# Strided pairs for the moving operand and the bank: the fp32r pass of a GRU's gate matmuls on TensorE

## The chip, the cores and the metric

The kernel runs on one NeuronCore of a Trainium2 chip. The metric is the device time of one launch in microseconds (us); lower is better. A second number that appears below is the span of the profiled execution, from its first to its last instruction.

## The reference

64 graphs of 256 nodes with 256 features each. Two layers, both of the form `x = x + layer(relu(layernorm(x)))`:

```python
# layer 0: gated graph network, 3 rounds, A = (adj != 0)
for i in range(3):
    m = h @ weight[i]
    aggr = A.T @ m                      # per graph
    gi, gh = aggr @ w_ih.T + b_ih, h @ w_hh.T + b_hh
    r, z = sigmoid(gi_r + gh_r), sigmoid(gi_z + gh_z)
    n = tanh(gi_n + r * gh_n)
    h = (1 - z) * n + z * h
# layer 1: graph attention, one head
h = relu(layernorm(x)) @ W.T
e = leaky_relu(h @ a_left [:, None] + h @ a_right [None, :])
x = x + softmax(where(adj == 0, -1e9, e)) @ h
```

All inputs and the output are fp32 (`adj` is int32).

## The kernel before

**Tiling.** Two graphs make a pair, so a tile is 128 partitions by 512 columns (2 graphs of 256 nodes). There are 32 pairs. The features lie on the partitions, in two blocks of 128 (`DB` = 2), and the nodes along the free dimension.

**Three passes in place of fp32.** A value `v` is split into three tiles by `split16` (L662 to L679) or `limbs`: a tile of the class `round` with dtype fp32r (4 bytes an element[...]), and two fp16 tiles of the class `half` (the remainder, and a scaled copy). The weights are split in the same way in the setup: `fac[m]` is fp32r, `low[m]` holds two fp16 parts; `m` is "hh" for the hidden weights, 0, 1 or 2 for the product of `weight[i]` and the input weights, "W" for the attention layer. A product is then one fp32r matmul (j = 0) and two fp16 matmuls (j = 1, 2) for each block of 128 contracted features, all added up in one PSUM bank of 512 fp32 columns.

**The gates.** `gate` (L704) takes a bank and runs `passes` (L698) for the terms it is given: `hs`, the split of the state h, against `fac_hh` and `low_hh`, and `gs`, the split of the aggregated neighbours g, against the factor of the round. For one pair and one round there are, for each of the two output blocks, the gates r (h and g), nh (h), ni (g) and z (h and g), so 6 terms, each with 2 contracted blocks and 3 passes: 12 fp32r matmuls with h and 12 with g for a pair and round. Over 32 pairs and 3 rounds this gives 1152 of each. In the last pair the rounds 1 and 2 are done for each graph by itself, with twice as many matmuls of 256 columns. The profile counts 1128 of 512 columns and 48 of 256 for h, and as many for g. The line that issues them is L701:

```python
return [(j, lambda start, j=j, kb=kb: nc.tensor.matmul(bank.t[:, cols], fs(j, kb), s[kb][j].t[:, cols], start=start, stop=True,
                                                       skip_group_check=True)) for kb in range(DB) for j in range(3)]
```

In this call the first operand is the bank that is written, the second is the stationary operand (128 columns of a factor), and the third is the moving operand, streamed column by column from SBUF. All three are contiguous runs in each partition.

**Who reads the bank.** ScalarE takes r and z with a tanh (L859, L872), scales nh in place (L723); VectorE takes nh and ni (L864, L867). They read the bank contiguously.

**Other fp32r matmuls.** The propagation along A (`prop`, L840) and the attention layer (`mix` L1005, `project` L1024) use fp32r and 16-bit passes too. The plain fp32 matmuls are few: the setup (L639) and the last pair.

**Order.** `Plan.run` is a list scheduler in Python: it places every operation by estimated cost, priorities and hand-set leads (`LEAD`), with pools of buffers for the classes (28 `full`, 22 `round`, 40 `half`, 8 `bank`). It decides the order of the instructions on each engine when the kernel is built. The costs that it uses for a gate, `PASS` = 233 ns for an fp32r pass of 512 columns and `PASS16` = 216 ns for a 16-bit one, are constants of the kernel.

**A copy that reads from two places.** For the transposes through DMA, `dma_turn` and `join` (L744 to L748) move 16-bit halves of fp32 values. `join` is a ScalarE copy of 1024 elements of 2 bytes that reads alternately from two planes of the source and writes contiguously:

```python
dst.t.bitcast(U16).rearrange("p (j n b) -> p j n b", j=2, b=2),
src.t.bitcast(U16).rearrange(f"p ({order}) -> p j n b", j=2, b=2)   # order: "b j n" or "j b n"
```

Of the kernel before, what the change touches and what calls it, by code (L numbers as in the profile page):

```python
# [372 lines left out]
def tile_gated_gnn_then_gat(  # L373
# [39 lines left out]
    nc = tc.nc  # L413
# [281 lines left out]
    def columns(part):  # L695
        return slice(part[0] * N, (part[-1] + 1) * N)

    def passes(bank, cols, m, es, s, first):  # L698

        fs = lambda j, kb: fac[m][:, kb, es] if j == 0 else low[m][:, j - 1, kb, es]  # L700
        return [(j, lambda start, j=j, kb=kb: nc.tensor.matmul(bank.t[:, cols], fs(j, kb), s[kb][j].t[:, cols], start=start, stop=True,  # L701
                                                               skip_group_check=True)) for kb in range(DB) for j in range(3)]

    def gate(name, e, terms, tops, apart=False, bias=None, part=ALL):  # L704

        bank = Buf("bank")
        half = e // 3
        cols, cost, cost16 = columns(part), PASS if len(part) == 2 else PROP, PASS16 if len(part) == 2 else PROP16

        def go(terms, first):  # L710
            seq = [q for m, s in terms for q in passes(bank, cols, m, ts(e, P), s, first)]
            seq.sort(key=lambda q: ((1, 2, 0) if narrow[0] else (0, 1, 2)).index(q[0]))
            for n, (j, run) in enumerate(seq):
                run(first and n == 0)

        for ts_ in [terms[:1], terms[1:]] if apart and len(terms) > 1 else [terms]:
            early = len(ts_) < len(terms) and ts_[0] is terms[0]
            tops.append(pe(name + " top" + str(early)[0], 2 * (cost + 2 * cost16) * len(ts_),
                           lambda ts_=ts_: go(ts_, ts_[0] is terms[0]), mixed=True,
                           r=[(s[kb][j], part) for _, s in ts_ for kb in range(DB) for j in range(3)] + [  # L720
                               (f"fac{m}", tuple((kb, half, j) for kb in range(DB) for j in range(2))) for m, _ in ts_], w=[(bank, ONE)]))
        if bias is not None:
            act(name + " scale", fit(575, part), lambda: nc.scalar.activation(  # L723
                bank.t[:, cols], bank.t[:, cols], AF.Identity, bias=bias), r=[("b_nh", ONE)], w=[(bank, ONE)])
        return bank
# [395 lines left out]
```

## Time and profile before

| | |
|---|---|
| median of 2 runs | 1945.63 us (1944.67 to 1946.6) |
| the profiled execution | 1943.53 us, of which its span is 1941.7 us |
| TensorE busy (PE, matmuls) | 1930.5 us, 99% of the span |
| weight loads (PEld) | 1216.4 us, 63% |
| VectorE (DVE) | 1650.8 us, 85% |
| ScalarE (ACT) | 1593.6 us, 82% |
| GpSimd (POOL) | 171.2 us, 9% |
| granted TensorE clock | 0.999 of full speed |

How to read the profile's rows: "L701 PE MATMUL bank<-round,fac_hh 128\*128 128x512 f32" is a matmul issued by line 701, which writes a bank from a moving `round` tile and the stationary `fac_hh`; fp32r operands show as f32. Behind the bar stand the busy time of the group, the mean duration of one instruction in ns, and the idle time of the engine ahead of it. The duration of a matmul contains the way through the pipeline, so durations of neighbours overlap; the price of a matmul in a dense stream is the distance between starts, which the timeline shows.

### The profile page before, as it was taken

The numbers are of one execution on the slowest core, as the hardware profiler recorded it, in microseconds if no ns is written. First come the engines' busy times: TensorE is split into PE (matmuls) and PEld (weight loads), VectorE is DVE, ScalarE is ACT, GpSimd is POOL, SyncE is SP. The second block draws the span as 40 slices with busy tenths as digits, with TensorE's granted clock in tenths as the row PEclk, the third lists the DMA queues.
The fourth block names the chain that finished last, engine by engine and source line by source line (L and its number), as shares of the span: only waits on it lengthen the run. The fifth ranks groups of instructions, "written<-read, shape, count | busy, mean of one in ns | idle before, by whom it ended". The sixth has DMA issues, their size and how long they took to land.

```text
span 1941.7 us, 31443 instructions
## 1 busy us (share of the span) xinstructions
PE 1930.5 (99%) x10288; PEld 1216.4 (63%) x10288; DVE 1650.8 (85%) x3972; ACT 1593.6 (82%) x2789; POOL 171.2 (9%) x262
## 2 busy tenths in 40 slices
PE   9999999999999999999999999999999999999998
PEld 6655666666666666666666666666666666666677
DVE  7677889888889888898888898888898888988887
ACT  6567888888888888888888888888888888888876
POOL 2001011010011010110010110101110101100000
PEclk9999999999999999999999999999999999999999
DMA  4138766676665676765666665677656765657543
GB/s 142 24 92 129 136 126 126 112 143 136 136 127 113 128 141 134 136 127 108 138 141 136 123 128 115 142 136 129 135 115 127 141 136 133 122 113 140 119 77 71
DMA packets 734469, 239.43 MB, mean 123 GB/s; under 512 B 658256, under 2 KB 734304, under 8 KB 734304
## 3 DMA queue, kind: packets, MB, share of 16 engines
q1 hardware_dynamic: 734272, 237.41, 62.3%
q8 instruction: 80, 1.31, 0.3%
q14 instruction: 85, 0.70, 0.1%
q10 hardware_dynamic: 32, 0.01, 0.0%
HBM read 61.09 MB, written 16.84 MB: 40 GB/s over the span
## 4 chain that ended last, share of the span: by engine, by line
PE 96%; DVE 1%; DMA 1%; ACT 1%; issue 0%; SPq 0%; ACTq 0%; DVEq 0%
PE bank L701 77%; PE bank L840 9%; PE bank L1024 4%; PE bank L1005 4%; PE bank L639 1%; DMA full<-full 0%; DMA x<-in_x_dram 0%; DMA full<-line 0%; DMA full<-in_L_gnn_w_hh_dram 0%; DVE full L939 0%; DVE small L761 0%; PE bank L1066 0%; PE bank L911 0%; PE bank L1074 0%; PE bank L1035 0%
## 5 line engine op out<-in xcount | busy, mean ns | idle before, releaser
L701 PE MATMUL bank<-half,low_hh 128*128 128x512 f16 (+1 forms) x2352 | 623.3, 376 | 0.1
L701 PE MATMUL bank<-half,low 128*128 128x512 f16 (+1 forms) x2352 | 616.2, 376 | 0.0
L701 PE MATMUL bank<-round,fac_hh 128*128 128x512 f32 (+1 forms) x1176 | 404.3, 437 | 0.0
L746 ACT COPY full<-full 128x1024 uint16<-128x1024 uint16 x304 | 350.5, 1164 | 54.3 <-DMA full<-full 50.0
L701 PE MATMUL bank<-round,fac 128*128 128x512 f32 (+1 forms) x1176 | 394.1, 426 | 0.1
L701 PEld LDWEIGHTS <-low 128*128 128x128 f16 x2352 | 216.8, 98 | 261.5 <-issue 44.1
L701 PEld LDWEIGHTS <-low_hh 128*128 128x128 f16 x2352 | 206.3, 98 | 259.9 <-issue 79.8
L671 DVE SCALAR_TENSOR_TENSOR half<-bank,round 128x512 f16<-128x512 f32 (+1 forms) x254 | 171.7, 685 | 99.5 <-ACT round L669 84.0
L701 PEld LDWEIGHTS bank<-round,fac_hh 128*128 128x128 f32 x1176 | 217.0, 189 | 62.6
L701 PEld LDWEIGHTS bank<-round,fac 128*128 128x128 f32 x1176 | 215.5, 189 | 58.0 <-ACT round L669 0.4
L768 POOL TENSOR_TENSOR small<-small,nhalf 128x2 f32<-128x2 f32 x128 | 100.1, 783 | 1709.2 <-DVE small L766 1705.0
L859 ACT ACTIVATE full<-bank,b_rz 128x512 f32<-128x512 f32 (+1 forms) x196 | 132.3, 675 | 98.3 <-PE bank L701 97.9
L674 ACT ACTIVATE half<-bank 128x512 f16<-128x512 f32 (+1 forms) x254 | 151.2, 595 | 49.0 <-PE bank L1005 28.8
L872 ACT ACTIVATE full<-bank,b_rz 128x512 f32<-128x512 f32 (+1 forms) x196 | 132.2, 674 | 52.2 <-PE bank L701 50.9
L671 DVE SCALAR_TENSOR_TENSOR half<-full,round 128x512 f16<-128x512 f32 (+1 forms) x254 | 169.4, 680 | 5.0 <-ACT round L669 2.4
L864 DVE SCALAR_TENSOR_TENSOR full<-full,bank 128x512 f32<-128x512 f32 (+1 forms) x196 | 131.9, 673 | 40.1 <-ACT full L859 39.4
L723 ACT ACTIVATE bank<-bank,b_nh 128x512 f32<-128x512 f32 (+1 forms) x196 | 127.1, 649 | 44.2 <-PE bank L701 44.1
L669 ACT ACTIVATE round<-full 128x512 fp32r<-128x512 f32 (+1 forms) x254 | 152.7, 629 | 11.2 <-DVE full L880 10.3
L878 DVE SCALAR_TENSOR_TENSOR full<-full,full 128x512 f32<-128x512 f32 (+1 forms) x196 | 132.4, 676 | 33.1 <-ACT full L872 32.3
L688 DVE SCALAR_TENSOR_TENSOR half<-full,round 128x512 f16<-128x512 f32 x184 | 126.2, 687 | 25.0 <-ACT round L687 24.9
L669 ACT ACTIVATE round<-bank 128x512 fp32r<-128x512 f32 (+1 forms) x254 | 144.5, 598 | 1.0 <-PE bank L840 0.8
L876 DVE TENSOR_TENSOR full<-full,full 128x512 f32<-128x512 f32 (+1 forms) x196 | 130.6, 678 | 17.0 <-ACT full L869 17.0
(114 smaller groups left out, 2547.4 us busy)
## 6 DMA issues: line engine op xcount, KB each, us to landing
full<-full SPq DMA_DIRECT2D x484, 128.0 KB, 3.4
x<-in_x_dram SPq DMA_DIRECT2D x64, 256.0 KB, 3.1
adj<-in_adj_dram SPq DMA_DIRECT2D x64, 256.0 KB, 4.7
full<-in_x_dram SPq DMA_DIRECT2D x64, 256.0 KB, 4.9
full<-full SPq DMA_DIRECT2D x248, 64.0 KB, 2.5
out_dram<-full SPq DMA_DIRECT2D x62, 256.0 KB, 4.0
full<-line SPq DMA_DIRECT2D x62, 128.0 KB, 4.5
full<-full SPq DMA_TRANSPOSE x304, 3.2
```

The lines of the kernel that those rows point to most:

```text
L669: act(f"{name} 0{of}", cut(A512 if bank else C512), lambda: nc.scalar.activation(v0.t[:, cols], v.t[:, cols], AF.Copy, scale=up), r=[(v, h ...
L671: dve_(f"{name} 1{of}", cut(V512), lambda: nc.vector.scalar_tensor_tensor(v1.t[:, cols], v.t[:, cols], up, v0.t[:, cols].bitcast(F32), op0 ...
L674: act(f"{name} d{of}", cut(A512), lambda: nc.scalar.activation(vd.t[:, cols], v.t[:, cols], AF.Copy, scale=up * unit), r=[(v, has)], w=[(v ...
L701: return [(j, lambda start, j=j, kb=kb: nc.tensor.matmul(bank.t[:, cols], fs(j, kb), s[kb][j].t[:, cols], start=start, stop=True, skip_gro ...
L723: act(name + " scale", fit(575, part), lambda: nc.scalar.activation(bank.t[:, cols], bank.t[:, cols], AF.Identity, bias=bias), r=[("b_nh", ...
L746: act(name, 1065, lambda: nc.scalar.copy(dst.t.bitcast(U16).rearrange("p (j n b) -> p j n b", j=2, b=2), src.t.bitcast(U16).rearrange(f"p ...
L840: nc.tensor.matmul(pa.t[:, ts(g, N)], b, m[:, ts(sb, N)], start=(n == 0), stop=True, skip_group_check=True)
L859: act(f"r {db}{of}", fit(575, part), lambda b=r_, k=pr, db=db, cols=cols: nc.scalar.activation(b.t[:, cols], k.t[:, cols], AF.Tanh, bias=b ...
L864: dve(f"u {db}{of}", fit(S512, part), lambda u=u, k=ph, b=r_, cols=cols: nc.vector.scalar_tensor_tensor(u.t[:, cols], b.t[:, cols], 1.0, k ...
L872: act(f"z {db}{of}", fit(575, part), lambda b=z_, k=pz, db=db, cols=cols: nc.scalar.activation(b.t[:, cols], k.t[:, cols], AF.Tanh, bias=b ...
L876: dve2(f"d sub {db}{of}", fit(V512, part), lambda u=u, d=d, cols=cols: nc.vector.tensor_sub(d.t[:, cols], d.t[:, cols], u.t[:, cols]), r=[ ...
L878: dve2(f"d mul {db}{of}", fit(V512, part), lambda d=d, b=z_, cols=cols: nc.vector.scalar_tensor_tensor(d.t[:, cols], b.t[:, cols], 1.0, d. ...
```

## The change

The matmuls with j = 0 in `passes` (fp32r by fp32r) stream the moving tile in another order of columns and write the bank's columns in that same order, so that each column of the result lands where it did before. The 16-bit passes, the weights, and every reader of the bank stay as they are.

```diff
+    WEFT = {"hh": "p (l q e) -> p q l e", 0: "p (l q e) -> p q l e", 1: "p (l q e) -> p q l e", 2: "p (q l e) -> p l q e"}
+    STEP = {"hh": 4, 0: 4, 1: 8, 2: 2}
+
     def passes(bank, cols, m, es, s, first):
 
+        weft = lambda t, m, j: t.rearrange(WEFT[m], q=STEP[m], e=2) if j == 0 else t
         fs = lambda j, kb: fac[m][:, kb, es] if j == 0 else low[m][:, j - 1, kb, es]
-        return [(j, lambda start, j=j, kb=kb: nc.tensor.matmul(bank.t[:, cols], fs(j, kb), s[kb][j].t[:, cols], start=start, stop=True,
+        return [(j, lambda start, j=j, kb=kb: nc.tensor.matmul(
+            weft(bank.t[:, cols], m, j), fs(j, kb), weft(s[kb][j].t[:, cols], m, j), start=start, stop=True,
                                                                skip_group_check=True)) for kb in range(DB) for j in range(3)]
```

In all cases the innermost run is a pair of neighbouring elements (8 bytes). What follows a pair differs:

| m | pattern of 512 columns | distance to the next pair | matmuls of 512 / of 256 columns |
|---|---|---|---|
| hh | 4 x 64 x 2 | 32 bytes | 1128 / 48 |
| 0 | 4 x 64 x 2 | 32 bytes | 384 / 0 |
| 1 | 8 x 32 x 2 | 64 bytes | 372 / 24 |
| 2 | 128 x 2 x 2 | 1024 bytes forth, then back to the pair beside the first | 372 / 24 |

(With 256 columns the counts in the middle halve, and the distance for m = 2 is 512 bytes.) In the first three patterns the row of pairs is run through from end to end, and then again 8 bytes further on. Every engine has the same instructions in the same order as before; the scheduler's costs are not touched.

## The prediction

> **What bounds the kernel now.** I read the page's busy times first, then the chain that ended last, then the waits of TensorE, and last the timeline for the price of one matmul.
>
> ```profile
> PE 1930.5 (99%) x10288; PEld 1216.4 (63%) x10288; DVE 1650.8 (85%) x3972; ACT 1593.6 (82%) x2789; POOL 171.2 (9%) x262
> ...
> PE 96%; DVE 1%; DMA 1%; ACT 1%; issue 0%; SPq 0%; ACTq 0%; DVEq 0%
> ...
> L701 PE MATMUL bank<-round,fac_hh 128*128 128x512 f32 (+1 forms) x1176 | 404.3, 437 | 0.0
> L746 ACT COPY full<-full 128x1024 uint16<-128x1024 uint16 x304 | 350.5, 1164 | 54.3 <-DMA full<-full 50.0
> L701 PE MATMUL bank<-round,fac 128*128 128x512 f32 (+1 forms) x1176 | 394.1, 426 | 0.1
> ...
> L669 ACT ACTIVATE round<-full 128x512 fp32r<-128x512 f32 (+1 forms) x254 | 152.7, 629 | 11.2 <-DVE full L880 10.3
> ```
>
> Busy share alone would not do, since matmuls overlap in it. But the chain agrees: 96% of the span is TensorE following TensorE, 77.0% of it L701. The two fp32r rows are the 2352 matmuls that the change touches; their idle time is 0.0 and 0.1 us.
>
> The waits of TensorE, all of the span (us, times, longest):
>
> ```profile
> PE bank L1024 <- ACT round L669: 2.9, 1, 2.9
> PE bank L527 <- POOL ident masks.py:199: 1.4, 1, 1.4
> ```
>
> The nine entries of that answer sum to under 8 us. There is no slack on TensorE: a nanosecond more per matmul goes into the time nearly in full, and the other engines (85% and 82% busy) follow.
>
> The price of one matmul, from the timeline (start, length of the row, what):
>
> ```profile
> 593.27 0.82 PE L701 MATMUL bank<-round,fac_hh 128*128 128x512 f32 x2
> 593.93 0.63 PE L701 MATMUL bank<-round,fac 128*128 128x512 f32 x2
> 594.39 0.63 PE L1024 MATMUL bank<-fac_W,round 128*128 128x256 f32 x4
> 594.87 1.05 PE L1024 MATMUL bank<-low_W,half 128*128 128x256 f16 x8
> 595.75 0.59 PE L701 MATMUL bank<-half,low_hh 128*128 128x512 f16 x2
> 596.18 0.59 PE L701 MATMUL bank<-half,low 128*128 128x512 f16 x2
> ```
>
> From start to start: two fp16 matmuls of 512 columns take 596.18 - 595.75 = 0.43, so 0.215 each; two fp32r ones 594.39 - 593.93 = 0.46, so 0.23. (The first fp32r row after 16-bit ones is recorded early and isn't used.) With 256 columns: fp16 0.88 / 8 = 0.11, fp32r 0.48 / 4 = 0.12. A longer stretch confirms this: the chain has "325.36 16.04 PE bank L701 x72", and the groups of that window are 48 fp16 and 24 fp32r matmuls: (16.04 - 48 x 0.2155) / 24 = 0.237, changes of kind included. I take 0.233 (0.12 for 256 columns). So the contiguous fp32r stream already runs some 8% below the fp16 stream, and in proportion to its columns[...].
>
> [...]
>
> **What a new line costs, from the trace.** `join` (L746) reads 1024 elements of 2 bytes, alternately from two places[...]. It takes 1164 ns. A contiguous copy of as many elements: L669 takes 632 ns for 512 and 418 for 256 columns (groups by form), a slope of 0.836 ns an element, so 632 + 512 x 0.836 = 1060. [...] TensorE takes an element in 0.42 ns. [...] the alternative, that the fp32r stream is held back by its bytes[...], fits the 8% as well.
>
> **The change part by part.**
> 1. Nothing is removed; instruction counts and order are the same on all engines. The split tiles, the weights (190 ns a load against 233 of a matmul, hidden) and the readers of the bank are untouched.
> 2. hh, 0 and 1: [...] Count: 1128 + 384 + 372 = 1884 of the first kind, 48 + 24 = 72 of the second. 1884 x 0.230 = 433.3, and 72 x 0.115 = 8.3. Bounds: below, no extra at all (0), or a gain of 0.018 for each if the 8% came from the order and vanished; above, 0.230.
> 3. Round 2: pairs go back and forth between two places, as `join` does[...]. I take 0. Upper bound[...]: 372 x 0.230 + 24 x 0.115 = 88.3.
> 4. The bank: [...] I take 0 beside item 2[...]. [...]
> 5. What hides it: nothing on TensorE. The last 23 us of the chain lie mostly on VectorE, so some of the 8.3 us may be covered there; I leave them in.
>
> Sum against the profiled execution's own time: 1943.5 + 433.3 + 8.3 = 2385.1. The median of the runs stands 2.1 higher, so 2387.
>
> **The rivals.**
> - *Pairs are enough (not slower).* [...] Place: every fp32r matmul of L701. Price 0 each: 1945.6. [...] if the 8% vanish, 2256 x 0.018 = 41 less, 1905. [...] For: over its 1024 alternating reads `join` loses only 104 of 1060 ns[...]. [...]
> - *One step a line.* [...] 1884 x 0.104 + 72 x 0.052 = 200, so 2146; with round 2 as well, 2186. [...] Against: TensorE has half the time for an element.
> - *The array's own half rate.* The pairs go at exactly half of fp16's pace, 0.43 instead of 0.233: 1884 x 0.197 + 72 x 0.10 = 378, so 2324; with round 2, 2404. This is inside the forecast's own range.
> - *The bank is worse than the reading*[...]. Nothing in the profile gives a price; if it costs double again, over 2480.
>
> **How the numbers follow.** Doubling of the lines, with or without round 2: 0.48, own range 2310 to 2480. One step a line: 0.17 (2100 to 2200). Pairs are enough: 0.31 (1905 to 1985, mostly at 1946). The bank worse: 0.04. To leave out no more than 2 in 10 the range must reach from the rival at 1946 to the forecast's upper end: 1940 to 2480. Faster by over 2% (about what a measurement of this kernel can tell from no change) would need all of the 8% back and more: 0.01. Within 2%: 0.30. Slower: 0.69.
>
> **What would show it.** In the changed profile the distance between starts of the fp32r matmuls of hh, 0 and 1 should be 0.43 to 0.47 us, those of round 2 (the third large block of gates of a pair) should stay near 0.233, the fp16 ones 0.215, and `prop`, `mix` and `project` 0.12. PE stays at 99%, DVE and ACT fall to about 70% and 66% (1650.8 and 1593.6 over 2385). The prediction is wrong if hh stays at 0.233 (pairs are enough), if it is near 0.34 (one step), or if round 2 is slowed like the others.

## The result and the profile after

The changed kernel takes 2398.43 us (median of 2 runs, 2397.81 to 2399.04) against 1945.63: a ratio of 1.2327, with an interval of 1.2274 to 1.238. The forecast was 2387 us, slower with a chance of 0.69. The profiled execution took 2399.04 us with a span of 2397.2, so the span grew by 455.5 us.

The page after, with busy times, the chain, and the gates' groups (now at L705):

```profile
PE 2389.9 (100%) x10288; PEld 1258.4 (52%) x10288; DVE 1667.9 (70%) x3972; ACT 1626.6 (68%) x2789; POOL 170.8 (7%) x262
...
PE 99%; DMA 0%; DVE 0%; SPq 0%; issue 0%; ACT 0%; ACTq 0%
...
L705 PE MATMUL bank<-round,fac_hh 128*128 128x512 f32 (+1 forms) x1176 | 668.9, 681 | 0.0
L705 PE MATMUL bank<-half,low_hh 128*128 128x512 f16 (+1 forms) x2352 | 628.5, 379 | 0.0
L705 PE MATMUL bank<-half,low 128*128 128x512 f16 (+1 forms) x2352 | 618.9, 377 | 0.0
L705 PE MATMUL bank<-round,fac 128*128 128x512 f32 (+1 forms) x1176 | 601.4, 616 | 0.0
```

The two fp32r groups grew from 404.3 to 668.9 and from 394.1 to 601.4 us; the fp16 groups hardly moved. TensorE's busy time grew by 459.4 us and its idle time fell from 11.2 to 7.3, which together is the 455.5. The other engines have the same work spread over more time (70% and 68%). So the loss lies in the 2352 matmuls that the change touches, and on the path that sets the end.

The timeline after (start, length, what) around two places; the first lies in round 2, the second at the passage from round 1 to round 0:

```profile
919.49 1.09 PE L705 MATMUL bank<-round,fac_hh 128*128 128x512 f32 x2
920.40 0.84 PE L705 MATMUL bank<-round,fac 128*128 128x512 f32 x2
921.08 0.40 PE L705 MATMUL bank<-half,low_hh 128*128 128x512 f16 x1
...
952.74 1.06 PE L705 MATMUL bank<-round,fac 128*128 128x512 f32 x2
953.61 1.12 PE L705 MATMUL bank<-round,fac_hh 128*128 128x512 f32 x2
954.55 1.92 PE L705 MATMUL bank<-half,low_hh 128*128 128x512 f16 x8
956.12 1.27 PE L705 MATMUL bank<-round,fac_hh 128*128 128x512 f32 x2
957.19 1.12 PE L705 MATMUL bank<-round,fac 128*128 128x512 f32 x2
958.13 0.63 PE L705 MATMUL bank<-half,low 128*128 128x512 f16 x2
```

From start to start, for one matmul: hh (32 bytes) (920.40 - 919.49) / 2 = 0.455 and (954.55 - 953.61) / 2 = 0.47; g in round 0 (32 bytes) (958.13 - 957.19) / 2 = 0.47; g in round 1 (64 bytes) (953.61 - 952.74) / 2 = 0.435; g in round 2 (back and forth) (921.08 - 920.40) / 2 = 0.34. Before, all were at 0.23.

### The profile page after: what moved, and what is told of

Read it like the earlier page. It is cut to its first block, busy times and chain, and to the rows that moved or that the text cites. A ratio compares the mean times of both kernels' runs of the same rounds, so it can differ in the third digit from the quotient of the medians.

```text
span 2397.2 us, 31442 instructions
## 1 busy us (share of the span) xinstructions
PE 2389.9 (100%) x10288; PEld 1258.4 (52%) x10288; DVE 1667.9 (70%) x3972; ACT 1626.6 (68%) x2789; POOL 170.8 (7%) x262
## 4 chain that ended last, share of the span: by engine, by line
PE 99%; DMA 0%; DVE 0%; SPq 0%; issue 0%; ACT 0%; ACTq 0%
PE bank L705 83%; PE bank L845 7%; PE bank L1029 3%; PE bank L1010 3%; PE bank L639 0%; DMA x<-in_x_dram 0%; PE bank L1018 0%; DMA full<-in_L_gnn_w_hh_dram 0%; PE bank L1071 0%; PE bank L916 0%; PE bank L1079 0%; PE bank L1040 0%; PE bank L656 0%; PE bank L898 0%; DVE small L766 0%; SPq L555 0%
## 5 line engine op out<-in xcount | busy, mean ns | idle before, releaser
L705 PE MATMUL bank<-round,fac_hh 128*128 128x512 f32 (+1 forms) x1176 | 668.9, 681 | 0.0
L705 PE MATMUL bank<-half,low_hh 128*128 128x512 f16 (+1 forms) x2352 | 628.5, 379 | 0.0
L705 PE MATMUL bank<-half,low 128*128 128x512 f16 (+1 forms) x2352 | 618.9, 377 | 0.0
L705 PE MATMUL bank<-round,fac 128*128 128x512 f32 (+1 forms) x1176 | 601.4, 616 | 0.0
L705 PEld LDWEIGHTS <-low_hh 128*128 128x128 f16 x2352 | 214.8, 104 | 374.7 <-issue 194.2
L705 PEld LDWEIGHTS <-low 128*128 128x128 f16 x2352 | 220.5, 100 | 319.0 <-issue 101.1
L705 PEld LDWEIGHTS bank<-round,fac 128*128 128x128 f32 x1176 | 228.2, 198 | 167.0 <-issue 126.8
L877 ACT ACTIVATE full<-bank,b_rz 128x512 f32<-128x512 f32 (+1 forms) x196 | 133.0, 679 | 267.6 <-PE bank L705 267.6
L705 PEld LDWEIGHTS bank<-round,fac_hh 128*128 128x128 f32 x1176 | 225.4, 196 | 139.3 <-issue 75.5
L872 DVE TENSOR_TENSOR full<-full,bank 128x512 f32<-128x512 f32 (+1 forms) x196 | 131.8, 674 | 79.8 <-PE bank L705 76.3
L874 ACT ACTIVATE full<-full,vec 128x512 f32<-128x512 f32 (+1 forms) x196 | 138.9, 711 | 38.2 <-DVE full L872 36.3
```

Of the source, the lines that this page charges most:

```text
L705: return [(j, lambda start, j=j, kb=kb: nc.tensor.matmul(weft(bank.t[:, cols], m, j), fs(j, kb), weft(s[kb][j].t[:, cols], m, j), start=st ...
L872: dve(f"u add {db}{of}", fit(V512, part), lambda u=u, k=pn, cols=cols: nc.vector.tensor_add(u.t[:, cols], u.t[:, cols], k.t[:, cols]), r=[ ...
L874: act(f"tanh {db}{of}", fit(615, part), lambda u=u, en=en, cols=cols: nc.scalar.activation(u.t[:, cols], u.t[:, cols], AF.Tanh, bias=b_i[: ...
L877: act(f"z {db}{of}", fit(575, part), lambda b=z_, k=pz, db=db, cols=cols: nc.scalar.activation(b.t[:, cols], k.t[:, cols], AF.Tanh, bias=b ...
```

## The experiments

In all kernels below the factors carry names of their own: `fac_hh`, and `fac_first`, `fac_second`, `fac_third` for 0, 1 and 2, so that one run prices four patterns in groups of their own (the matmuls with h, and those with g in rounds 0, 1 and 2). The price per matmul is read as: busy time of the group, less that of the same group with contiguous reading, over the count. (At the seams of groups records overlap, so small differences of this reading are uncertain by a few ns: contiguous `fac_first` reads 132.0 us and, beside the strided fp16 passes below, 133.0, 0.003 each.) The contiguous figures come from the write-only kernel: 393.9 us for `fac_hh` (1128 matmuls of 512 columns), 132.0 for `fac_first` (384), 123.9 for `fac_second` (372) and 128.8 for `fac_third` (372). A pattern is written as in the change, `F` for `"p (l q e) -> p q l e"` and `A` for `"p (q l e) -> p l q e"`, followed by q and e. "Runs" of a pattern are the neighbouring elements that it takes at a visit, its "step" is the distance from one run to the next. Contiguous, a matmul of 512 columns takes 0.215 us from start to start in fp16, and 0.017 more in fp32r, 0.232 (medians of the durations before: 379 and 396 ns).

The expectations speak of lines. A line is here a stretch of the row whose first element costs the stream extra time and whose others come with it. That each pair costs a line of its own was supposed before any run and is not shown by the profile before; what the runs show of a line's price and length is put together after the single elements.

**Reading alone.**

```diff
+    MOVING = {"hh": (F, 4, 2), 0: (F, 4, 2), 1: (F, 8, 2), 2: (A, 2, 2)}
+    BANK = {"hh": None, 0: None, 1: None, 2: None}
-            weft(bank.t[:, cols], m, j), fs(j, kb), weft(s[kb][j].t[:, cols], m, j), start=start, stop=True,
+            weft(bank.t[:, cols], BANK[m], j), fs(j, kb), weft(s[kb][j].t[:, cols], MOVING[m], j), start=start, stop=True,
```

> Only the moving operand of the fp32r gate matmuls is read in the order of the change; the bank is written contiguously, so the columns of these products land in other places than the reference asks for. Theory 'lines of SBUF'[...]: all of the loss stays, about 2400 us, starts 0.46 us apart for the 32-byte step and 0.33 for round 2. Rival 'bank' (the order of writing in PSUM costs it): the loss goes, 1946 us, starts 0.233 apart. If both halve the rate on their own, about 2400 here and in the write-only kernel.

Measured: 2398.43 us, ratio 1.2347 (1.2326 to 1.2368). The groups by form:

```profile
L711 PE MATMUL bank<-round,fac_hh 128*128 128x512 f32 x1128 | 653.0, 692 | 0.0
...
L711 PE MATMUL bank<-round,fac_first 128*128 128x512 f32 x384 | 222.3, 678 | 0.0
...
L711 PE MATMUL bank<-round,fac_second 128*128 128x512 f32 x372 | 200.2, 649 | 0.0
...
L711 PE MATMUL bank<-round,fac_third 128*128 128x512 f32 x372 | 165.6, 548 | 0.0
```

More per matmul: 0.230 us for hh, 0.235 for 0, 0.205 for 1; `fac_third` (round 2) 0.099. All of the loss is in the reading.

**Writing alone.** `MOVING` and `BANK` of the kernel above are exchanged.

> The counterpart: the moving operand is read contiguously, the bank is written in the order of the change, so the columns land in other places. Theory 'lines of SBUF': 1946 us within 0.5%, starts 0.233 us apart. Rival 'bank': about 2400 us, 0.46 apart for the 32-byte step. If the bank costs only beside round 2's back and forth: 1944 + 372 x 0.097 = 1980.

Measured: 1944.08 us, ratio 1.0001 (0.9992 to 1.0009).

```profile
L711 PE MATMUL bank<-half,low_hh 128*128 128x512 f16 x2256 | 608.0, 381 | 0.0
L711 PE MATMUL bank<-round,fac_hh 128*128 128x512 f32 x1128 | 393.9, 442 | 0.0
...
L711 PE MATMUL bank<-round,fac_first 128*128 128x512 f32 x384 | 132.0, 427 | 0.0
L711 PE MATMUL bank<-round,fac_third 128*128 128x512 f32 x372 | 128.8, 440 | 0.0
...
L711 PE MATMUL bank<-round,fac_second 128*128 128x512 f32 x372 | 123.9, 427 | 0.0
```

The 393.9 is that of the kernel before, to the digit. Writing the bank in pairs at steps of 32, 64 or 1024 bytes costs nothing here. The rival "bank" falls.

**Runs of four elements.**

```diff
-    MOVING = BANK = {"hh": (F, 4, 2), 0: (F, 4, 2), 1: (F, 8, 2), 2: (A, 2, 2)}
+    MOVING = BANK = {"hh": (F, 2, 4), 0: (F, 4, 4), 1: (F, 8, 4), 2: (A, 2, 4)}
```

> As the change, with runs of four elements (16 bytes) in place of pairs: steps of 32, 64 and 128 bytes for hh, 0 and 1, back and forth between two places for 2; reading and writing alike. Theory 'lines of SBUF': [...] 1946 us (starts 0.233), at most 1% more. Rival 'any step off the next element costs': half of the pairs' extra for half as many breaks, about 0.35 us a matmul, 2170 us. Rival 'the bank by its step': as the change, 2400.

Measured: 1949.9 us in one run. Per matmul against contiguous: hh (32 bytes) 392.5 us for the group, -0.001; 0 (64 bytes) 127.7, -0.011; 1 (128 bytes) 128.4, +0.012; 2 (back and forth) 135.5, +0.018.

```profile
L711 PE MATMUL bank<-round,fac_hh 128*128 128x512 f32 x1128 | 392.5, 442 | 0.0
...
L711 PE MATMUL bank<-round,fac_first 128*128 128x512 f32 x384 | 127.7, 415 | 0.0
```

A strided stream as such costs next to nothing: with 16 bytes at a time instead of 8 at most 0.018 us a matmul is left of the loss, and at a step of 64 bytes the stream is even quicker than the contiguous one. That was not expected.

**Pairs at other distances.**

```diff
+    MOVING = BANK = {"hh": (F, 2, 2), 0: (F, 16, 2), 1: (F, 32, 2), 2: (F, 64, 2)}
```

> Pairs at other distances: 16 bytes for hh, 128, 256 and 512 bytes for 0, 1 and 2; reading and writing alike. Theory 'lines of SBUF': every pair still fetches a line, whatever the distance, so starts 0.43 to 0.46 us apart for all four, round 2 included, and 1944 + 1128 x 0.229 + 1128 x (0.20 to 0.229) = 2430 to 2460 us. Rival 'even and odd parts'[...]: hh falls to 0.233, so 2170 to 2205 us.

Measured: 2460.12 us in one run. More per matmul: 16 bytes 0.223, 128 bytes 0.240, 256 bytes 0.270, 512 bytes 0.215.

```profile
L711 PE MATMUL bank<-round,fac_hh 128*128 128x512 f32 x1128 | 645.5, 685 | 0.0
```

Pairs about double the matmul at every distance tried (0.215 to 0.270 more on 0.232), the step of 16 bytes included; the rival "even and odd parts" falls. The four prices differ by up to 0.055, but each distance was tried on other matmuls, so this run doesn't say that the distance makes the difference.

**Pairs from several places in turn.**

```diff
+    MOVING = BANK = {"hh": (A, 2, 2), 0: (A, 4, 2), 1: (A, 8, 2), 2: (A, 16, 2)}
```

> Pairs taken in turn from 2 places (hh, 1024 bytes apart), 4 places (0, 512 apart), 8 (1) and 16 (2), and then from the next pair at each place; reading and writing alike. If the two lines last used are kept, 2 places cost 0.33 us a matmul (as round 2 in the change) and 4, 8 and 16 places the full 0.43 to 0.49: 1944 + 1128 x 0.097 + 1128 x 0.22 = 2300 us. If more lines are kept, 4 places (or more) are at 0.33 too: 2050 to 2200. Rival 'no line is kept, jumps of 1024 bytes happen to be cheap': 0.33 for 2 places, and no step between 2 and 4 that goes with the number of places.

Measured: 2311.93 us in one run. More per matmul: 2 places 0.098, 4 places 0.223, 8 places 0.269, 16 places 0.210.

```profile
L711 PE MATMUL bank<-round,fac_hh 128*128 128x512 f32 x1128 | 504.7, 549 | 0.0
...
L711 PE MATMUL bank<-round,fac_first 128*128 128x512 f32 x384 | 217.6, 666 | 0.0
...
L711 PE MATMUL bank<-round,fac_hh 128*128 128x256 f32 x48 | 12.7, 363 | 0.0
```

The jump in price lies between 2 and 4 places. I read it so, as an estimate from the 0.098 and the 0.223: a line is still there if one other was used in between, and gone if three were. The rival "jumps of 1024 bytes happen to be cheap" falls by the matmuls of 256 columns in the same run: their two places lie 512 bytes apart, and they cost (12.7 - 10.4) / 48 = 0.048 more than contiguous, again about half of the price of pairs for 256 columns (0.115), while four places at the same 512 bytes cost the whole of it.

Three of these patterns are those of the run before in other words. A row of 512 columns has 2048 bytes, so pairs at a step of 512, 256 or 128 bytes come from 4, 8 or 16 places in turn. The price of one and the same pattern was thus taken twice: 0.215 (with `fac_third`) and 0.223 (with `fac_first`) for 512 bytes, 0.270 and 0.269 (both with `fac_second`) for 256, 0.240 (with `fac_first`) and 0.210 (with `fac_third`) for 128. What sets the last 0.03 is therefore not the pattern alone.

**The fp16 passes strided.** The fp32r passes stay contiguous; `weft` acts for j = 1 and 2, with

```diff
+    MOVING = BANK = {"hh": (F, 8, 2), 0: (F, 4, 4), 1: (F, 2, 8), 2: (A, 2, 2)}
```

> The fp32r passes are contiguous; in their place both fp16 passes of the gates are strided: pairs of 4 bytes at a step of 32 bytes for hh, runs of four (8 bytes) at 32 bytes for 0, runs of eight (16 bytes) at 32 bytes for 1, pairs back and forth between two places for 2. Theory 'lines of SBUF at 1.67 ns': what counts is the number of lines, not of bytes: hh fetches 256 lines, 0.43 to 0.46 us in place of 0.216; 0 fetches 128, 0.216 to 0.232; 1 fetches 64, 0.216; 2 between 0.216 and 0.33. Sum: 1944 + 2256 x (0.214 to 0.245) + up to 12 + up to 85 = 2430 to 2590 us. [...]

Measured: 2548.66 us in one run.

```profile
L711 PE MATMUL bank<-half,low_hh 128*128 128x512 f16 x2256 | 1152.6, 633 | 0.0
...
L711 PE MATMUL bank<-half,low_third 128*128 128x512 f16 x744 | 240.8, 439 | 0.0
L711 PE MATMUL bank<-half,low_first 128*128 128x512 f16 x768 | 216.4, 396 | 0.0
L711 PE MATMUL bank<-half,low_second 128*128 128x512 f16 x744 | 203.9, 383 | 0.0
```

Contiguous, these groups are at 608.0, 196.6, 203.4 and 201.7 us. More per matmul: pairs (4 bytes) at 32 bytes 0.241; runs of four (8 bytes) 0.017; runs of eight (16 bytes) 0.003; pairs back and forth 0.059. (`fac_hh`, which is contiguous here, also shows more busy time, 439.3 against 393.9 us. I read that as overlap of records with the slower fp16 matmuls: the fp16 groups alone grew by 617 us, the 256-column ones included, which is more than the 603.4 us that the time grew over 1945.22 before on this chip.) Runs of 8 bytes double the fp32r stream and leave the fp16 stream nearly alone, while runs of two elements double both. So it isn't bytes that count, but elements: by the runs so far, two at a visit are too few (0.230 and 0.241 more), and four are enough (at most 0.018 more). The next run narrows this down.

**Single elements, reading alone.**

```diff
+    MOVING = {"hh": (F, 2, 1), 0: (F, 4, 1), 1: (F, 8, 1), 2: (A, 2, 1)}
+    BANK = {"hh": None, 0: None, 1: None, 2: None}
```

> Single fp32r elements, in the reading alone (the bank is written contiguously, so the columns land in other places): steps of 8, 16 and 32 bytes for hh, 0 and 1, single elements back and forth between two places for 2. Theory 'lines at 1.67 to 1.8 ns': hh fetches 256 lines[...], 0.43 to 0.46 us; 0 and 1 fetch 512, 0.86 to 0.92 us; 2 keeps its lines, 0.33. Sum: 1944 + 1128 x 0.22 + 756 x 0.65 + 372 x 0.1 = 2720 us. Rival 'what is not the next element costs the same once, pair or single': 0.46 for 0 and 1 as well, 2400 us.

Measured: 2346.93 us in one run, 370 less than my theory said.

```profile
L711 PE MATMUL bank<-round,fac_hh 128*128 128x512 f32 x1128 | 642.6, 682 | 0.0
...
L711 PE MATMUL bank<-round,fac_first 128*128 128x512 f32 x384 | 222.3, 678 | 0.0
...
L711 PE MATMUL bank<-round,fac_second 128*128 128x512 f32 x372 | 199.9, 649 | 0.0
...
L711 PE MATMUL bank<-round,fac_third 128*128 128x512 f32 x372 | 124.5, 430 | 0.0
```

Singles at 16 bytes (`fac_first`) cost 0.235 more, at 32 bytes (`fac_second`) 0.204: what the pairs cost at 32 and 64 bytes in these groups (222.3 and 200.2 us), though twice as many places are visited. Singles at 8 bytes (`fac_hh`) cost 0.220, as the pairs at 16 bytes did (0.223). And single elements back and forth between two places (`fac_third`) cost nothing; they are 0.012 quicker than the contiguous stream. A price per line visited, the theory so far, can't say this. Nor can the rival of the expectation, by which what is not the next element costs the same each time: from two places in turn no element is the next one.

What can is a model, an estimate of mine from these runs: the columns enter two at a time, and the first and the second of each two are fetched each for itself. I call them two streams, one of the even and one of the odd columns. Each delivers an element in a step of 0.84 ns, two columns at the pace of the fp16 stream (0.215 / 256), and a new line takes it two steps, 1.68 ns: the pairs of the change take 0.435 to 0.47 us, 1.70 to 1.84 ns for each two columns. The length of a line is read from the same runs: in contiguous fp32r the elements of one stream lie 8 bytes apart and keep the pace (0.232 us), in pairs at 16 bytes they lie 16 apart and cost 0.223 more, so I put it at 16 bytes, four fp32r elements. Pairs at 16, 32 and 64 bytes and singles at 8, 16 and 32 bytes then give each stream the same walk, a new line for every element at a step of 16, 32 and 64 bytes; this is why their prices agree three times over. Runs of four give each stream two elements to the line. Singles from two places give each a contiguous run of its own, four elements to the line. The 0.017 by which fp16 in runs of 8 bytes is slower fits too: there each stream has two elements to the line, as in contiguous fp32r, which stands 0.017 above contiguous fp16 (0.232 against 0.215).

**The same elements in two orders.** To try that theory against the one before, the fp32r matmuls of `prop` (256 columns, 768 of them; the gates are as before the change) read two elements from each 16 bytes of the tile's row, 128 lines of the model:

```diff
-                            nc.tensor.matmul(pa.t[:, ts(g, N)], b, m[:, ts(sb, N)], start=(n == 0), stop=True, skip_group_check=True)
+                            nc.tensor.matmul(pa.t[:, ts(g, N)], b, of_block(m, sb, part, lo), start=(n == 0), stop=True, skip_group_check=True)
+                        # of_block, for the fp32r part; for the 16-bit part as before
+                        return m.rearrange("p (l h q e) -> p q l e h", h=2, q=2, e=2)[:, sb]     # A0 B0 A1 B1
+                        return m.rearrange("p (l h q e) -> p q l h e", h=2, q=2, e=2)[:, sb]     # A0 A1 B0 B1, the other kernel
```

> The gates are as before the change. The 768 fp32r matmuls of the propagation read, from all lines of the tile, one half of each (so half of the columns twice over two matmuls' places; the columns are others than the reference asks for): in the order A0 B0 A1 B1, A and B neighbouring lines, then the next two lines. Theory 'two streams' (odd and even columns are fetched each for itself, a line costs each two steps of 0.83 ns): each stream takes two elements in turn from its line, 128 steps of columns, 0.109 to 0.12 us as before, 1946 us. Theory 'one stream, 1.7 to 1.8 ns a line': 128 lines for 256 columns, 0.23 us, 768 x 0.113 = 87 us more, 2032 us.

> The same elements as in the kernel before it, with the same part of the computation changed, in the order A0 A1 B0 B1. Theory 'two streams': each stream needs another line for every element, 0.216 to 0.23 us, 1944 + 768 x (0.097 to 0.113) = 2018 to 2032 us. Theory 'one stream': 128 lines[...], the same 0.23 and 2032 us. If instead both orders stay at 0.117, lines aren't what counts and both are at 1946.

Measured: 1945.23 us for A0 B0 A1 B1 and 2026.11 for A0 A1 B0 B1, one run each, against 1947.04 before on the same chip. The lines of `prop` from the one and the other, as minimum / median / maximum of the durations in ns:

```profile
L845 PE MATMUL bank<-round,round x768: 277/278/363, 23.7 to 1914.0; 128*128 128x256 f32 x192
```

```profile
L845 PE MATMUL bank<-round,round x768: 388/421/472, 22.0 to 1995.0; 128*128 128x256 f32 x192
```

Against the first order the second adds 80.9 us over 768 matmuls, 0.105 each; the first adds nothing to the time before. The same elements, in the same groups of four columns, cost once or nearly twice by their order alone: once where, in the model, each stream takes its two elements in turn from one line. One stream with a price per line would have given 2032 for both.

**Longer runs.**

```diff
+    MOVING = BANK = {"hh": (F, 2, 8), 0: (F, 4, 8), 1: (F, 4, 16), 2: (F, 16, 4)}
```

> Longer runs of fp32r elements, reading and writing alike: 32 bytes at a step of 64 for hh, 32 bytes at 128 for 0, 64 bytes at 256 for 1, 16 bytes at 256 for 2. All fetch 128 lines, so by the number of lines alone all take 0.216 to 0.235 us, 1920 to 1950 us in sum. What is beyond 1.67 ns a line goes with the step by the runs so far (runs of 16 bytes: 0.232 at 32 bytes, 0.221 at 64, 0.243 at 128): if a step of 64 bytes is what helps, hh is at 0.221 to 0.232; if a step of 256 hurts, 2 is at 0.245 or more, and 1 between.

Measured: 1958.59 us in one run. Per matmul against contiguous: 32 bytes at 64: -0.001 (392.7 us for the group); 32 at 128: -0.003; 64 at 256: +0.005; 16 at 256: +0.043. The number of lines alone doesn't settle what is left. In the same group, `fac_third`, 16 bytes at a step of 256 cost 0.043, and the next run has 16 bytes at 64 at 0.008 below contiguous, so the step has a part in it. Since reading and writing had the same step here, and the writing alone was never tried at 128, 256 or 512 bytes, the run can't say whether the step hurts the reading or the writing.

**A version that beats both.** Runs of four at 64 bytes for all fp32r gate matmuls, reading and writing alike:

```diff
+    MOVING = BANK = {"hh": (F, 4, 4), 0: (F, 4, 4), 1: (F, 4, 4), 2: (F, 4, 4)}
```

> All fp32r gate matmuls in runs of four elements (16 bytes) at a step of 64 bytes, reading and writing alike; this pattern took 0.221 us against 0.232 contiguous where it was tried, on the matmuls of g in the first round. If it is the pattern, 2256 x 0.011 = 25 us go: 1919 us, ratio 0.987. Rival 'it was the tiles of g in that round that happened to lie well': 384 x 0.011 = 4 us, 1940, ratio 0.998.

Measured: 1928.36 us against 1947.04, ratio 0.9904 (0.9887 to 0.992).

```profile
L711 PE MATMUL bank<-round,fac_hh 128*128 128x512 f32 x1128 | 382.9, 432 | 0.0
...
L711 PE MATMUL bank<-round,fac_first 128*128 128x512 f32 x384 | 128.8, 418 | 0.0
L711 PE MATMUL bank<-round,fac_third 128*128 128x512 f32 x372 | 125.7, 431 | 0.0
...
L711 PE MATMUL bank<-round,fac_second 128*128 128x512 f32 x372 | 120.1, 416 | 0.0
```

Each group is 8 to 10 ns a matmul below contiguous, (393.9 + 132.0 + 128.8 + 123.9) - (382.9 + 128.8 + 125.7 + 120.1) = 21.1 us in sum. It is the pattern and not one round's tiles, though a little less than the 11 ns expected: 1% of the kernel, a small gain, but the interval stays clear of 1.

The same pattern also in the propagation and the projection (`bank` and moving operand, fp32r passes only, 256 columns):

```diff
-nc.tensor.matmul(pa.t[:, ts(g, N)], b, m[:, ts(sb, N)], ...
+nc.tensor.matmul(fours(pa.t[:, ts(g, N)], part is not lo), b, fours(m[:, ts(sb, N)], part is not lo), ...
```

(`fours` is the pattern `F` with q = 4 and e = 4; the projection is changed in the same way.)

> As the kernel before it, and the fp32r matmuls of 256 columns in the propagation and in the projection of the attention layer in the same pattern. If the pattern takes the stream to 1.7 ns a line: 0.117 falls to 0.112, (768 + 240) x 0.005 = 5 us more, 1914 us, ratio 0.984; with the rival 1940 as well. The second block of 256 columns or the adjacency tiles may lie otherwise: between 1912 and 1922.

Measured: 1927.88 us, ratio 0.9907 (0.9892 to 0.9922): no more than the gates alone. The 5 us expected are not there in the time: the groups of `prop` and `project` fell by 2.6 and 0.9 us (125.1 to 122.5, 39.0 to 38.1), the idle time of TensorE is 1.3 us longer than with the gates alone (14.9 against 13.6), and what remains is less than the four runs differ among themselves.

## Why the prediction was right

**The bound.** Right: TensorE had no slack, and the extra went into the time nearly in full, 455.5 us of span.

**Item 2, the price of a pair.** 0.230 us more was forecast for hh, 0 and 1. Measured (reading alone): 0.230 for hh, 0.235 for 0, 0.205 for 1. For the 48 narrow matmuls of hh the group went from 10.4 to 15.9 us, 0.115 each as forecast. Round 1 was over-priced by 372 x 0.025 = 9 us. Single elements that walk at the same step in each stream cost the same there (0.204), but why 64 bytes are cheaper than 32 no run tells.

**The reason behind the price.** Half right. The 0.230, about the matmul's own time once more, was the author's estimate, on the thought that a new line costs two of the stream's steps and that contiguous fp32r already pays this. The profile before shows neither; `join` shows only that alternate reading took ScalarE 1164 ns against 1060. The runs fit the two steps: the cheapest pairs take 0.435 / 256 = 1.70 ns for each two columns, where the dense fp16 stream takes 0.215 / 256 = 0.84. The alternative that the prediction left open, that contiguous fp32r is held back by its bytes, falls: the same bytes went 8 to 11 ns quicker in runs of 16 bytes at 64, and 12 ns quicker as singles from two places. But the forecast thought of one stream with a price per line. The singles (2346.93 us where it gave 2720) and the two orders in `prop` (1945.23 and 2026.11 where it gave 2032 for both) refute this. The pairs have the right price in both pictures, because in the model a pair lies in one line and gives either stream one element of it; that the number agreed was luck as far as the picture goes, and no proof of it.

**Item 3, round 2.** Wrong. It was put at 0 on the author's estimate that going back and forth calls for no more lines than contiguous reading, with 88.3 us as the bound. Measured 36.8 us (165.6 - 128.8), 0.099 a matmul: about half of the price of a pair, so the sign that the prediction named for itself, round 2 slowed like the others, came true by half. That a line is kept fits the run over several places (2 places 0.098, 4 places 0.223). What is still paid has the size of one step for each line of the model: 128 x 0.84 = 0.108, measured 0.099, and for fp16 back and forth 64 x 0.84 = 0.054, measured 0.059. That is an estimate that fits, not a test. I used the row of `join` to price a rival and not the one part of the change that reads in turn from two places. Taken column by column the patterns differ, though: `join` takes single elements in turn, and single fp32r elements in this order cost TensorE nothing (124.5 us for the group against 128.8). They are alike only if each of the model's two streams is set beside the one of ScalarE.

**Item 4, the bank.** Right: 0, with an interval of 0.9992 to 1.0009, for pairs at steps of 32, 64 and 1024 bytes; no run here has single elements in the bank. In the reading, two elements in turn from a line nearly keep the pace if they are counted for each stream (0.011 us less to 0.043 more). Counted over the columns, as the rival "pairs are enough" did, two are too few (0.20 to 0.27 more).

**The sum.** 2385.1 was forecast for the profiled execution, 2399.0 came. The four fp32r groups grew by 259.1, 203.4, 5.5 and 4.0 us, 472 in sum, where 441.6 were forecast: round 2 was 37 too low, round 1 9 too high. Of the 472 only 455.5 show in the time, since the groups overlap at their seams (TensorE's busy time grew by 459.4) and its idle time fell by 3.9. So the total is as close as it is because these errors partly cancel; that is luck.

**The rivals.** "Pairs are enough" and "the bank is worse" fell with the first two runs. "One step a line", 0.104 a matmul, is wrong for the pairs that go straight on (0.205 to 0.235) and right for round 2 (0.099). "The array's own half rate", 0.43, is the spacing that round 1 shows, and 32 bytes lie 0.03 above it; but as a rate of the array for pairs it falls with the two orders in `prop`, where the order of the columns decides. Its sum with round 2 comes to 2324 + 372 x 0.197 + 24 x 0.10 = 2400 and not 2404. That this is the nearest of all figures to 2398.43 is luck too: it gives round 2 the whole price, where half was paid.

## What to carry to other kernels

When a moving operand is strided, count for the odd and the even columns separately how many elements in turn come from one line, by the model fitted here a stretch of 16 bytes. One to a line about doubles the matmul, in fp32r and in fp16 and at all distances tried (0.20 to 0.27 us more for 512 columns); where the streams go back and forth between two lines, it costs 0.06 to 0.10. Two to a line nearly keep the pace: from 0.011 less than contiguous to 0.043 more, by the pattern. So keep runs of four elements, or let two contiguous places alternate element by element. The same order in the bank did no harm in pairs at 32, 64 and 1024 bytes (1944.08 us against 1943.36). And where a row of the profile has an access pattern like that of an edit, try its price on the edit before a term is put at 0.

## What was not expected of the hardware

- A strided fp32r stream can be quicker than a contiguous one: 16 bytes at a step of 64 take 8 to 11 ns less of 232, 16 bytes at 256 take 43 ns more. Why steps of 64 bytes suit and 256 don't is open, and at 256 also whether it is the reading or the bank.
- Single fp32r elements taken in turn from two halves of a tile are read without any loss (124.5 us for the group against 128.8 contiguous).
- The bank may be written in pairs at steps of 32, 64 and 1024 bytes without a loss (1944.08 us against 1943.36).
- The two streams, their two steps and their lines of 16 bytes are a model that fits the runs up to some 0.05 us a matmul; that the order counts by every second column is shown by the two kernels of `prop`. The runs show times, not the circuit.
